# GAT attention weights from per-node exponentials gathered with the rows, in place of scores on TensorE

## The chip, the cores and the metric

The kernel runs on one core of a Trainium2 chip. The metric is the device time of one execution in microseconds (us), as the median of several runs. The engines are called PE (TensorE), DVE (VectorE), ACT (ScalarE), POOL (GpSimd) and SP (SyncE, which only issues DMAs here). All arithmetic of the tensors named below is in float32.

## What is computed

Four graph layers follow each other on x of shape (8, 2048, 128), with one adjacency matrix of 2048 x 2048 whose entries are 1 with probability 1/128, so that a node has 16 neighbours on average. Layers 0 and 1 are transformer blocks with attention over the neighbours. Layers 2 and 3 are GAT layers, and the change is in these:

```python
def _L2_gnn_ref(x, adj, W, a_src, a_dst, ln_gamma, ln_beta):   # _L3_gnn_ref is the same
    h = x @ W
    s_i = h @ a_src
    s_j = h @ a_dst
    e = s_i[:, :, None] + s_j[:, None, :]
    e = jnp.where(e >= 0, e, NEG_SLOPE * e)          # NEG_SLOPE = 0.2
    e = jnp.where(adj[None, :, :] == 0, -jnp.inf, e)
    att = jax.nn.softmax(e, axis=-1)
    att = jnp.nan_to_num(att, nan=0.0)
    out = jnp.einsum('bij,bjd->bid', att, h)
    y = out + x
    mu = jnp.mean(y, axis=-1, keepdims=True)
    var = jnp.mean((y - mu) ** 2, axis=-1, keepdims=True)
    return ln_gamma * (y - mu) * jax.lax.rsqrt(var + LN_EPS) + ln_beta
```

The weight of neighbour j for node i is the exponential of a leaky ReLU of s_i + s_j, divided by the sum of these over the neighbours.

## The kernel before

A first stage (`start`) finds the neighbours of every node and ranks the nodes by their number of neighbours. The 2048 nodes are then worked on in 16 tiles of 128 nodes of nearly equal degree. `CAPS` holds how many neighbour slots each tile has, from 30 down to 11; a slot that a node does not need is called padding. There are 277 slots in all.

For each layer there is a table in HBM with one row per node that holds what its neighbours need from it for all eight batches. For a GAT layer the row has 8 x 128 values of h and then 8 values s_j, 4128 bytes. One **gather** (L296, issued by POOL) brings the rows of one slot for the 128 nodes of a tile, each into its own partition of a kv buffer. A padding slot has an index past the end of the table (2N and more), and its row is skipped.

A GAT layer works on **chunks** of up to four slots of one tile (`pieces(t, 4)`), 75 per layer. `gat_chunk` is a generator; each `yield` ends one of its stages:

1. PE adds up the scores in PSUM: the mask of the padding slots (L654), s_i of the node itself (L658) and the gathered s_j (L662). ACT takes the exponential of the score (L667, tile wa) and of 0.2 times the score (L668, tile wb).
2. DVE takes the maximum of both, which is the exponential of the leaky ReLU: into a PSUM tile `pair` for DVE's own use (L670) and, for the last two batches, into an SBUF tile ws for ACT (L675).
3. DVE multiplies the rows of six batches by their weights (L681, one input in PSUM); ACT does the other two batches (L686).
4. DVE adds the second half of the slots to the first (L690); then PE adds the rows into the tile's accumulator by matmuls with the identity (L696).

Tile 0 has nodes with more neighbours than the others; two extra slots of that tile are shared out over idle partitions ("folded") and brought back by the matrices `spread` and `merge`.

When the last chunk of a tile is done, its **tail** starts: the sums of the weights and their reciprocals (`reciprocal_sums`, L388 to L395), the scaled output (L565), the residual (L706 to L714), the normalisation (`normed`: squares on ACT, L404; a power on POOL, L409; a scale on ACT, L413), and either the projection to the next layer's table row (`project`, L443 to L466) with its scatter by POOL (`put_rows`, L417), or in layer 3 a scale and a shift on DVE (L731, L732) and a store by POOL (L734). Tails are generators too, advanced by one stage in each `slot()`.

Every engine works through its instructions in the order in which the program issues them. That order is written out in `layer`. In iteration i a GAT layer issues the gathers of chunk i + 3, then the scores of chunk i + 1, the products of chunk i - 1, a slot, the maxima of chunk i, a slot, the addition and the matmuls of chunk i - 2, and a slot. Six kv buffers are used in turn, so the gathers of chunk i + 3 go into the buffer of chunk i - 3 and wait until its matmuls are done. A layer's first gathers wait for the last rows of its table.

After layer 3 `verdict` checks on DVE that no list overflowed and no sum left its range. If one did, a general path (`general_path`) computes everything anew.

Of the kernel before, what the change touches and what calls it, by code (L numbers as in the profile page):

```python
# [17 lines left out]
P = 128  # L18
# [11 lines left out]
CHUNK = 4 * NB * (D + 1)  # L30
KVB = 6
AHEAD = 3
# [10 lines left out]
SUM_MIN, SUM_MAX = 1e-25, 1e30  # L43

# [19 lines left out]
def sparse_path(ctx: ExitStack, tc: tile.TileContext, ins: dict, out: bass.AP, flag: bass.AP):  # L64
# [69 lines left out]
    lmask_bf = const.tile([P, sum(CAPS)], BF16, name="lmask_bf")  # L134
    first = [sum(CAPS[:t]) for t in range(NT)]
    s_own = const.tile([P, NT, B], F32, name="s_own")
# [142 lines left out]
    def width(l):  # L279
        return NB * (2 * D if l < 2 else D + 1)  # L280

    tables = [dram.tile([N, width(l)], F32, name=f"table{l}") for l in range(4)]
# [12 lines left out]
    def gather(l, at, dst):  # L295
        nc.gpsimd.indirect_dma_start(  # L296
            out=dst, out_offset=None, in_=tables[l][:, :],
            in_offset=bass.IndirectOffsetOnAxis(ap=lists[:, at : at + 1], axis=0),
            bounds_check=N - 1, oob_is_err=False,
        )  # L300
# [24 lines left out]
    def find_lists(t):  # L325
# [18 lines left out]
        if t == 0:  # L344
# [19 lines left out]
        nc.vector.tensor_copy(lmask_bf[:, sl], lmask[:, sl])  # L364
# [3 lines left out]
            far[:, :s], top[:, :s], 0.0, float(2 * N), op0=ALU.is_equal, op1=ALU.mult  # L368
# [54 lines left out]
    def project(l, i, xT, rows, t):  # L423
# [18 lines left out]
        else:  # L442
# [22 lines left out]
            nc.scalar.copy(rows[:, NB * D + i : NB * D + i + 4], ps[:, :, 0])  # L465
            nc.scalar.copy(s_own[:, t, i : i + 4], ps[:, :, 1])  # L466
# [177 lines left out]
    def gat_chunk(l, c):  # L644
        box, t, k, ns = c["box"], c["t"], c["k"], c["ns"]
        if k == 0:
            box["acc"] = pacc.tile([P, NB // 4, 512], F32, tag="acc", name="acc")
            at, n = (0 if t % 2 == 0 else 512 - NB * CAPS[t]), CAPS[t]
            box["w"] = pair[:, at : at + NB * n].rearrange("p (s b) -> p s b", b=NB)
        acc, w = box["acc"], box["w"]  # L650
        hs = c["buf"]
        e = misc()[:, : ns * NB].rearrange("p (s b) -> p s b", b=NB)
        at = first[t] + k
        nc.tensor.matmul(  # L654
            e, ident_bf, lmask_bf[:, at : at + ns, None].to_broadcast([P, ns, NB]),
            start=True, stop=False,
        )
        nc.tensor.matmul(  # L658
            e, spread if c["folded"] else ident, s_own[:, t, None, :].to_broadcast([P, ns, NB]),
            start=False, stop=False,  # L660
        )
        nc.tensor.matmul(e, ident, hs[:, :, NB * D :], start=False, stop=True)  # L662

        wc = w[:, k : k + ns, :]
        wa = small.tile([P, 4, NB], F32, tag="wa", name="wa", bufs=3)
        wb = small.tile([P, 4, NB], F32, tag="wb", name="wb", bufs=3)
        nc.scalar.activation(wa[:, :ns, :], e, AF.Exp)  # L667
        nc.scalar.activation(wb[:, :ns, :], e, AF.Exp, scale=SLOPE)  # L668
        yield
        nc.vector.tensor_max(wc, wa[:, :ns, :], wb[:, :ns, :])  # L670
        if c["folded"]:
            box["wf"] = small.tile([P, FOLD, NB], F32, tag="wf", name="wf", bufs=1)
            nc.vector.tensor_max(box["wf"], wa[:, :ns, :], wb[:, :ns, :])
        ws = small.tile([P, 4, SCALED], F32, tag="ws", name="ws", bufs=3)
        nc.vector.tensor_max(  # L675
            ws[:, :ns, :], wa[:, :ns, NB - SCALED :], wb[:, :ns, NB - SCALED :]
        )
        yield
        hv = hs[:, :, : NB * D].rearrange("p s (b c) -> p s b c", b=NB)
        nv = NB - SCALED  # L680
        nc.vector.tensor_mul(  # L681
            hv[:, :, :nv, :], hv[:, :, :nv, :], wc[:, :, :nv, None].to_broadcast([P, ns, nv, D])
        )
        for i in range(ns):
            for b in range(nv, NB):
                nc.scalar.mul(hv[:, i, b, :], hv[:, i, b, :], ws[:, i, b - nv : b - nv + 1])  # L686
        yield
        left = -(-ns // 2)
        if ns > 1:
            nc.vector.tensor_add(hv[:, : ns - left], hv[:, : ns - left], hv[:, left:ns])  # L690
        yield
        if c["folded"]:
            folded_sums(box["wf"], box)
        for i in range(left):
            for j in range(NB // 4):
                nc.tensor.matmul(  # L696
                    acc[:, j, :], merge if c["folded"] else ident, hv[:, i, 4 * j : 4 * j + 4, :],
                    start=k + i == 0, stop=c["last"] and i == left - 1,
                )
        yield  # L700
# [41 lines left out]
    def start():  # L742
# [164 lines left out]
        for i in (3, 4, 5):  # L907
            nc.scalar.copy(bufs[i], nil.to_broadcast([P, CHUNK]))


    def verdict():
        ok = small.tile([P, 4], F32, tag="ok", name="ok", bufs=1)
# [7 lines left out]
        nc.vector.tensor_mul(ok[:, 0:1], ok[:, 0:1], ok[:, 2:3])  # L920
        pk = misc()
# [40 lines left out]
    def layer(l):  # L962
# [36 lines left out]
        for i in range(AHEAD):  # L999
            fetch(i)  # L1000
# [22 lines left out]
        if not att:  # L1023
            go(0)
        for i in range(n + 2):
            fetch(i + AHEAD)
# [24 lines left out]
            else:  # L1051


                go(i + 1)
                if is_last(i - 1):
                    sums(l, chunks[i - 1]["t"], chunks[i - 1]["box"])
                go(i - 1)
# [3 lines left out]
                go(i - 2, 2)  # L1061
                if is_last(i - 2):
                    end(i - 2)
# [534 lines left out]
```

## Time and profile before

| What | Value |
|---|---|
| median of 3 runs | 3482.68 us |
| lowest and highest | 3482.06 and 3488.56 us |
| the profiled execution, its own time | 3489.46 us |
| its span, first to last instruction | 3487.7 us |
| busy share of the span | PE 81%, DVE 87%, ACT 42%, POOL 61% |
| moved by DMA | 955.38 MB, mean 274 GB/s |
| layer 2, its gathers under way | 2325 to 2852 us |
| layer 3, its gathers under way | 2903 to 3425 us |

A row of the list of groups names the line of the kernel, the engine, the operation and its tiles (out<-in) with their shapes and the count; then come the busy time in us and the mean of one instruction in ns, and then the idle time of the engine just before these instructions, with what ended it. A row of the timeline has the start and the duration in us, and in brackets the idle time before. A row of the waits has the total in us, how many times, and the longest. "issue" is time in which an engine waited for nothing that the profile shows.

### The profile page before, as it was taken

The page shows a single profiled execution, that of the slowest core. Times are in us where ns is not written, and L with a number is a line of the kernel's source. Part 1 is how long each engine was busy: PE and PEld are TensorE (multiplying, and loading weights), DVE is VectorE, ACT ScalarE, POOL GpSimd, SP SyncE. Part 2 cuts the span into 40 slices and gives each one's busy share as a digit, 9 for nine tenths or more (in the row PEclk, how much of TensorE's full clock was granted, in tenths as well). Part 3 has the DMA queues.
Part 4 walks back from the last instruction along what each step waited for, and adds up shares of the span by engine and source line. Part 5 has one row for each costly group of instructions (what it writes and reads, how often), then busy time and mean ns, then how long its engine had stood idle before and what let it go on. Part 6 is the DMA issues. An engine that isn't in the chain of part 4 may idle for free. (4 is left out here: it accounts for less than half of the span.)

```text
span 3487.7 us, 36421 instructions
## 1 busy us (share of the span) xinstructions
PE 2838.8 (81%) x11364; PEld 1678.0 (48%) x11364; DVE 3033.3 (87%) x2545; ACT 1451.0 (42%) x5142; POOL 2117.5 (61%) x1441
## 2 busy tenths in 40 slices
PE   5657888889899966888888999958889895778786
PEld 4523454555555542445545555644555553434343
DVE  7789999999999839999999999928787764888885
ACT  5712333344444430233333344444555553444444
POOL 0054666666666432656666766537777755888874
PEclk9878999999999989999999999988999997988888
DMA  8486788878787457777887887638989856888883
GB/s 335 183 303 244 278 304 303 322 281 317 294 319 290 182 213 252 290 290 287 302 320 290 306 305 283 240 131 281 313 302 310 313 201 220 286 287 294 290 276 119
DMA packets 195892, 955.38 MB, mean 274 GB/s; under 512 B 33778, under 2 KB 35572, under 8 KB 124080
## 3 DMA queue, kind: packets, MB, share of 16 engines
q0 software_dynamic: 172352, 859.22, 69.0%
q1 hardware_dynamic: 18434, 75.51, 5.7%
q10 hardware_dynamic: 4904, 18.24, 1.4%
q8 instruction: 93, 1.52, 0.2%
q14 instruction: 109, 0.89, 0.1%
HBM read 934.86 MB, written 85.07 MB: 292 GB/s over the span
## 5 line engine op out<-in xcount | busy, mean ns | idle before, releaser
L296 POOL DMA_INDIRECT kv<-table,lists x1108 | 1614.4, 1457 | 553.9 <-issue 225.5
L546 PE MATMUL acc<-kv,ident 128*128 128x512 f32 x2200 | 1112.2, 636 | 255.7 <-DVE kv L536 255.5
L546 PEld LDWEIGHTS acc<-kv,ident 128*128 128x128 f32 x2200 | 414.2, 202 | 699.2 <-issue 370.4
L522 DVE TENSOR_TENSOR kv<-kv,q 128x2048 f32<-128x2048 f32 (+1 forms) x282 | 629.2, 2231 | 71.3 <-DMA kv<-table,lists 64.1
L525 DVE TENSOR_REDUCE sc<-kv 128x128 f32<-128x2048 f32 (+1 forms) x284 | 634.1, 2233 | 9.4
L409 POOL TENSOR_TENSOR rs<-ss,half 128x4 f32<-128x4 f32 x192 | 322.4, 1679 | 517.2 <-ACT n L404 510.0
L536 DVE TENSOR_TENSOR kv<-kv,w 128x2048 f32<-128x2048 f32 (+1 forms) x284 | 631.4, 2223 | 0.0
L696 PE MATMUL acc<-kv,ident 128*128 128x512 f32 x1184 | 605.6, 659 | 15.2 <-DVE kv L690 15.2
L404 ACT ACTIVATE n<-m,eps 128x128 f32<-128x128 f32 x768 | 271.5, 368 | 476.3 <-PE m L628 217.3
L681 DVE TENSOR_TENSOR kv<-kv,pair 128x3072 f32<-128x3072 f32 (+1 forms) x150 | 465.1, 3100 | 0.0
L531 ACT ACTIVATE w<-sc,lmask 128x64 f32<-128x64 f32 x554 | 164.4, 348 | 530.6 <-DVE sc L525 420.1
L696 PEld LDWEIGHTS acc<-kv,ident 128*128 128x128 f32 x1184 | 239.9, 213 | 272.1 <-issue 226.7
L690 DVE TENSOR_TENSOR kv<-kv 128x2048 f32<-128x2048 f32 (+1 forms) x150 | 296.5, 1977 | 85.3 <-ACT kv L686 83.3
L686 ACT ACTIVATE kv<-kv,ws 128x128 f32<-128x128 f32 x1108 | 339.1, 398 | 0.1
L413 ACT ACTIVATE n<-m,rs 128x128 f32<-128x128 f32 x768 | 218.3, 368 | 103.0 <-POOL rs L409 102.5
L667 ACT ACTIVATE wa<-m 128x32 f32<-128x32 f32 (+1 forms) x150 | 29.4, 196 | 494.2 <-PE m L662 494.2
L662 PE MATMUL m<-kv,ident 128*128 128x32 f32 (+1 forms) x300 | 62.1, 289 | 172.7 <-DMA kv<-table,lists 168.5
L404 ACT ACTIVATION_READ_ACCUMULATOR n<-m,eps 128x1 f32 x768 | 159.1, 207 | 0.0
L628 PE MATMUL m<-w_L_w,hT 128*128 128x128 f32 x1024 | 156.3, 275 | 0.0
L670 DVE TENSOR_TENSOR pair<-wa,wb 128x32 f32<-128x32 f32 (+1 forms) x150 | 29.9, 200 | 144.6 <-ACT wb L668 131.8
L417 POOL DMA_INDIRECT table<-rows,perm x48 | 77.8, 1620 | 110.1 <-ACT rows L441 51.6
L662 PEld LDWEIGHTS m<-kv,ident 128*128 128x128 f32 x300 | 49.2, 206 | 178.8 <-issue 150.1
(217 smaller groups left out, 3592.9 us busy)
## 6 DMA issues: line engine op xcount, KB each, us to landing
kept<-xT SPq DMA_DIRECT2D x48, 512.0 KB, 6.2
xT<-kept SPq DMA_DIRECT2D x48, 512.0 KB, 6.3
kv<-table,lists POOLq DMA_INDIRECT x1108, 6.5
kv<-in_adj_dram SPq DMA_DIRECT2D x16, 1024.0 KB, 7.0
table<-kv ACTq DMA_DIRECT2D x16, 1024.0 KB, 5.8
kv<-in_x_nodes_dram SPq DMA_DIRECT2D x16, 512.0 KB, 6.4
found<-cand POOLq DMA_DIRECT2D x16, 64.0 KB, 3.2
table<-rows,perm POOLq DMA_INDIRECT x48, 6.9
```

The source lines that it names most:

```text
L296: nc.gpsimd.indirect_dma_start(out=dst, out_offset=None, in_=tables[l][:, :], in_offset=bass.IndirectOffsetOnAxis(ap=lists[:, at : at + 1] ...
L404: nc.scalar.activation(dst[:, i, :], z[:, i, :], AF.Square, bias=eps, scale=D**-0.5, accum_out=ss[:, i : i + 1],)
L409: nc.gpsimd.tensor_tensor(rs, ss, half, op=ALU.pow)
L413: nc.scalar.mul(dst[:, i, :], z[:, i, :], rs[:, i : i + 1])
L522: nc.vector.tensor_mul(kk, kk, q[:, None].to_broadcast([P, ns, NB, D]))
L525: nc.vector.tensor_reduce(sc[:, :ns].rearrange("p s (b h) -> p (s b) h", h=NH), kk.rearrange("p s b (h j) -> p (s b) h j", h=NH), axis=AX. ...
L536: nc.vector.tensor_mul(vv, vv, w[:, k : k + ns, :].rearrange("p s (b h) -> p (s b) h", h=NH)[:, :, None, :] .to_broadcast([P, ns * NB, HD, ...
L546: nc.tensor.matmul(acc[:, j, :], merge if c["folded"] else ident, kv[:, i, 4 * j : 4 * j + 4, D:], start=k + i == 0, stop=c["last"] and i ...
L681: nc.vector.tensor_mul(hv[:, :, :nv, :], hv[:, :, :nv, :], wc[:, :, :nv, None].to_broadcast([P, ns, nv, D]))
L686: nc.scalar.mul(hv[:, i, b, :], hv[:, i, b, :], ws[:, i, b - nv : b - nv + 1])
L690: nc.vector.tensor_add(hv[:, : ns - left], hv[:, : ns - left], hv[:, left:ns])
L696: nc.tensor.matmul(acc[:, j, :], merge if c["folded"] else ident, hv[:, i, 4 * j : 4 * j + 4, :], start=k + i == 0, stop=c["last"] and i = ...
```

## The change

The exponential of a sum is a product of exponentials. Divided by exp(s_i), which is the same in all weights of a node and so drops out of the softmax, the weight is the larger of exp(s_j) and exp(0.2 s_j) exp(-0.8 s_i). The change puts exp(s_j) and exp(0.2 s_j) into the table row (8 + 8 values in place of 8, so 4160 bytes) and keeps exp(-0.8 s_i) of each node in SBUF (`own`). A chunk then multiplies the second gathered half by `own` on DVE and takes the maximum; PE and ACT have no part in the weights. The projection makes the exponentials, and `score` keeps the raw scores, so that `verdict` can check that none is beyond 80.

There is no mask any more. A padding slot now has the index N, and for the GAT tables row N exists, is filled with zeros once in `start`, and is read like any other row. In layers 0 and 1 row N is still past the end and skipped.

The chunk has one stage less, so the order in `layer` is new as well: in iteration i the gathers of chunk i + 4 are issued, then the maxima of chunk i, a slot, its products, a slot, the addition and the matmuls of chunk i - 1, and a slot.

```diff
-CHUNK = 4 * NB * (D + 1)
+CHUNK = 4 * NB * (D + 2)
-AHEAD = 3
+AHEAD = (3, 3, 4, 4)
+SCORE_MAX = 80.0
...
-    lmask_bf = const.tile([P, sum(CAPS)], BF16, name="lmask_bf")
-    s_own = const.tile([P, NT, B], F32, name="s_own")
+    own = const.tile([P, NT, B], F32, name="own")
+    score = const.tile([P, 2, NT, 2 * B], F32, name="score")
...
-        return NB * (2 * D if l < 2 else D + 1)
-    tables = [dram.tile([N, width(l)], F32, name=f"table{l}") for l in range(4)]
+        return NB * (2 * D if l < 2 else D + 2)
+    tables = [dram.tile([N + (l > 1), width(l)], F32, name=f"table{l}") for l in range(4)]
...
-            bounds_check=N - 1, oob_is_err=False,
+            bounds_check=N - (l < 2), oob_is_err=False,
...
-        nc.vector.tensor_copy(lmask_bf[:, sl], lmask[:, sl])
-            far[:, :s], top[:, :s], 0.0, float(2 * N), op0=ALU.is_equal, op1=ALU.mult
+            far[:, :s], top[:, :s], 0.0, float(N + 1), op0=ALU.is_equal, op1=ALU.mult
...
-            nc.scalar.copy(rows[:, NB * D + i : NB * D + i + 4], ps[:, :, 0])
-            nc.scalar.copy(s_own[:, t, i : i + 4], ps[:, :, 1])
+            at = NB * D + i
+            nc.scalar.activation(rows[:, at : at + 4], ps[:, :, 0], AF.Exp)
+            nc.scalar.activation(rows[:, at + NB : at + NB + 4], ps[:, :, 0], AF.Exp, scale=SLOPE)
+            nc.scalar.activation(own[:, t, i : i + 4], ps[:, :, 1], AF.Exp, scale=SLOPE - 1)
+            nc.scalar.copy(score[:, l - 2, t, 2 * i : 2 * i + 8], ps.rearrange("p b c -> p (b c)"))
...
     def gat_chunk(l, c):
         box, t, k, ns = c["box"], c["t"], c["k"], c["ns"]
+        mine = own[:, t, :]
+        if c["folded"]:
+            pf = misc()[:, :NB]
+            nc.tensor.matmul(pf, spread, mine, start=True, stop=True)
+            mine = small.tile([P, NB], F32, tag="mine", name="mine", bufs=1)
+            nc.scalar.copy(mine, pf)
+            yield
...
-        e = misc()[:, : ns * NB].rearrange("p (s b) -> p s b", b=NB)
-        at = first[t] + k
-        nc.tensor.matmul(
-            e, ident_bf, lmask_bf[:, at : at + ns, None].to_broadcast([P, ns, NB]),
-            start=True, stop=False,
-        )
-        nc.tensor.matmul(
-            e, spread if c["folded"] else ident, s_own[:, t, None, :].to_broadcast([P, ns, NB]),
-            start=False, stop=False,
-        )
-        nc.tensor.matmul(e, ident, hs[:, :, NB * D :], start=False, stop=True)
-
         wc = w[:, k : k + ns, :]
-        wa = small.tile([P, 4, NB], F32, tag="wa", name="wa", bufs=3)
-        wb = small.tile([P, 4, NB], F32, tag="wb", name="wb", bufs=3)
-        nc.scalar.activation(wa[:, :ns, :], e, AF.Exp)
-        nc.scalar.activation(wb[:, :ns, :], e, AF.Exp, scale=SLOPE)
-        yield
-        nc.vector.tensor_max(wc, wa[:, :ns, :], wb[:, :ns, :])
+        wa, wb = hs[:, :, NB * D : NB * (D + 1)], hs[:, :, NB * (D + 1) :]
+        nc.vector.tensor_mul(wb, wb, mine[:, None, :].to_broadcast([P, ns, NB]))
+        nc.vector.tensor_max(wc, wa, wb)
...
         nc.vector.tensor_max(
-            ws[:, :ns, :], wa[:, :ns, NB - SCALED :], wb[:, :ns, NB - SCALED :]
+            ws[:, :ns, :], wa[:, :, NB - SCALED :], wb[:, :, NB - SCALED :]
         )
...
+        for l in (2, 3):
+            nc.sync.dma_start(tables[l][N : N + 1, :], bufs[5][:1, : width(l)])
...
     def verdict():
-        ok = small.tile([P, 4], F32, tag="ok", name="ok", bufs=1)
+        ok = small.tile([P, 5], F32, tag="ok", name="ok", bufs=1)
+        every = score.rearrange("p a t b -> p (a t b)")
+        nc.vector.tensor_reduce(ok[:, 3:4], every, axis=AX.X, op=ALU.max)
+        nc.vector.tensor_reduce(ok[:, 4:5], every, axis=AX.X, op=ALU.min)
+        nc.vector.tensor_single_scalar(ok[:, 3:4], ok[:, 3:4], SCORE_MAX, op=ALU.is_le)
+        nc.vector.tensor_single_scalar(ok[:, 4:5], ok[:, 4:5], -SCORE_MAX, op=ALU.is_ge)
+        nc.vector.tensor_mul(ok[:, 3:4], ok[:, 3:4], ok[:, 4:5])
...
+        nc.vector.tensor_mul(ok[:, 0:1], ok[:, 0:1], ok[:, 3:4])
...
-        for i in range(AHEAD):
+        for i in range(AHEAD[l]):
...
-        if not att:
-            go(0)
         for i in range(n + 2):
-            fetch(i + AHEAD)
+            fetch(i + AHEAD[l])
...
-                go(i + 1)
+                if i + 1 < n and chunks[i + 1]["folded"]:
+                    go(i + 1)
                 if is_last(i - 1):
                     sums(l, chunks[i - 1]["t"], chunks[i - 1]["box"])
-                go(i - 1)
+                go(i)
                 slot()
                 go(i)
                 slot()
-                go(i - 2, 2)
-                if is_last(i - 2):
-                    end(i - 2)
+                go(i - 1, 2)
+                if is_last(i - 1):
+                    end(i - 1)
                 slot()
```

More of the change, by code (lines that the diff above doesn't have):

```diff
@@ L651, in gat_chunk @@
         hs = c["buf"]
-        e = misc()[:, : ns * NB].rearrange("p (s b) -> p s b", b=NB)
-        at = first[t] + k
-        nc.tensor.matmul(
-            e, ident_bf, lmask_bf[:, at : at + ns, None].to_broadcast([P, ns, NB]),
-            start=True, stop=False,
-        )
-        nc.tensor.matmul(
-            e, spread if c["folded"] else ident, s_own[:, t, None, :].to_broadcast([P, ns, NB]),
-            start=False, stop=False,
-        )
-        nc.tensor.matmul(e, ident, hs[:, :, NB * D :], start=False, stop=True)
-        wc = w[:, k : k + ns, :]
-        wa = small.tile([P, 4, NB], F32, tag="wa", name="wa", bufs=3)
-        wb = small.tile([P, 4, NB], F32, tag="wb", name="wb", bufs=3)
-        nc.scalar.activation(wa[:, :ns, :], e, AF.Exp)
-        nc.scalar.activation(wb[:, :ns, :], e, AF.Exp, scale=SLOPE)
-        yield
-        nc.vector.tensor_max(wc, wa[:, :ns, :], wb[:, :ns, :])
+        wc = w[:, k : k + ns, :]
+        wa, wb = hs[:, :, NB * D : NB * (D + 1)], hs[:, :, NB * (D + 1) :]
+        nc.vector.tensor_mul(wb, wb, mine[:, None, :].to_broadcast([P, ns, NB]))
+        nc.vector.tensor_max(wc, wa, wb)
         if c["folded"]:
             box["wf"] = small.tile([P, FOLD, NB], F32, tag="wf", name="wf", bufs=1)
-            nc.vector.tensor_max(box["wf"], wa[:, :ns, :], wb[:, :ns, :])
+            nc.vector.tensor_max(box["wf"], wa, wb)
         ws = small.tile([P, 4, SCALED], F32, tag="ws", name="ws", bufs=3)
         nc.vector.tensor_max(
-            ws[:, :ns, :], wa[:, :ns, NB - SCALED :], wb[:, :ns, NB - SCALED :]
+            ws[:, :ns, :], wa[:, :, NB - SCALED :], wb[:, :, NB - SCALED :]
         )
```

## The prediction

> **What bounds the kernel now.** Only the two GAT layers (l = 2, 3) are changed, so I first looked for their stretches. The table by window gives each engine's busy time, then the DMA share and GB/s. The second and third rows below are the layers while their gathers run (layer 2: 2325 to 2852 us, layer 3: 2903 to 3425 us); between and after them come the tails that close a layer.
>
> ```profile
> core 0: us, PE busy (x) PEld busy (x) DVE busy (x) ACT busy (x) POOL busy (x), PEclk, DMA share, GB/s
> 2325.00:2852.00 527.00, 445.44 (x1801) 260.98 (x1802) 403.65 (x366) 268.78 (x1103) 391.14 (x316) 0.91 0.87 298
> 2903.00:3425.00 522.00, 390.73 (x1216) 205.43 (x1215) 434.23 (x417) 237.01 (x985) 419.85 (x329) 0.86 0.86 287
> ```
>
> The obvious reading is the page's list of groups, where PE waits for gathers and ACT waits for PE's scores:
>
> ```profile
> L667 ACT ACTIVATE wa<-m 128x32 f32<-128x32 f32 (+1 forms) x150 | 29.4, 196 | 494.2 <-PE m L662 494.2
> L662 PE MATMUL m<-kv,ident 128*128 128x32 f32 (+1 forms) x300 | 62.1, 289 | 172.7 <-DMA kv<-table,lists 168.5
> ```
>
> It suggests that the scores are the brake. But a gather that lands late may have been issued late, so I read POOL, which issues every gather, in order of time (start, duration, and in brackets the idle time before), beside DVE:
>
> ```profile
> 3098.08 1.02 POOL L296 DMA_INDIRECT kv<-table,lists  x1 [0.30 <-issue]
> 3099.41 1.00 POOL L296 DMA_INDIRECT kv<-table,lists  x1 [0.30 <-issue]
> 3100.71 1.00 POOL L296 DMA_INDIRECT kv<-table,lists  x1 [0.30 <-PE acc L696]
> 3102.01 2.92 POOL L296 DMA_INDIRECT kv<-table,lists  x1 [0.30 <-issue]
> 3105.24 1.00 POOL L296 DMA_INDIRECT kv<-table,lists  x1 [0.30 <-issue]
> ```
> ```profile
> 3098.15 3.35 DVE L681 TENSOR_TENSOR kv<-kv,pair 128x3072 f32<-128x3072 f32 x1
> 3101.60 0.20 DVE L670 TENSOR_TENSOR pair<-wa,wb 128x32 f32<-128x32 f32 x1
> 3101.71 0.16 DVE L675 TENSOR_TENSOR ws<-wa,wb 128x8 f32<-128x8 f32 x1
> 3101.78 2.29 DVE L690 TENSOR_TENSOR kv<-kv 128x2048 f32<-128x2048 f32 x1
> ```
>
> Two things are to be seen. The gap before every POOL instruction is 0.30 us whatever is named as releaser: that is issue cost, not waiting. So POOL's true load is busy time plus 0.30 us per instruction: layer 3, 419.9 + 329 x 0.30 = 518.6 of 522 us (99%); layer 2, 391.1 + 316 x 0.30 = 485.9 of 527 us (92%). **POOL is full in layer 3 and nearly full in layer 2.** And the gather that starts inside the add L690 (both inputs in SBUF) takes 2.92 us instead of 1.00, while those under L681 (one input in the PSUM tile pair) are not stretched. In layer 2 POOL does wait, for a buffer:
>
> ```profile
> POOL kv L296 <- PE acc L696: 27.8, 21, 5.1
> ```
> ```profile
> L296 POOL DMA_INDIRECT kv<-table,lists x277 | 336.9, 1216 | 118.6 <-issue 59.1 <-PE acc L696 27.8 <-PE m L658 13.3
> ```
> ```profile
> L296 POOL DMA_INDIRECT kv<-table,lists x277 | 359.8, 1299 | 87.3 <-issue 55.7 <-PE acc L696 9.7 <-DMA table<-rows,perm 4.7
> ```
>
> The last two rows are layers 2 and 3; the mean gather is 83 ns longer in layer 3, because a POOL that never waits meets more of the adds.
>
> **What the Trainium skill says.** *SBUF — State Buffer*, "Who interferes with whom": a Vector instruction with two SBUF inputs and a GpSimd instruction that reads SBUF exclude each other. The trace agrees (2.92 against 1.00 us). *ScalarE: Activation LUTs*, "What ACT_TABLE_LOAD costs": a change to another table set costs some 2.66 us. The trace has a single table load, with Exp, Square and Relu all in use, so more Exps cost no load. *DMA: Bandwidth & Descriptors*, "Latency and other measured facts": rows that alias on HBM fell from 207 to 103 GB/s; I use it below for rows read from one address; no run here shows that case.
>
> **The change part by part.** Each layer has 75 chunks and 277 gathers.
>
> *PE and ACT lose the scores.* 150 x (0.18 + 0.28 + 0.29) us, L654, L658 and L662, is 112 us of PE. 150 x 2 x 0.196 is 59 us of ACT. The large effect is that their queues no longer stop for a gather with tails behind them. PE was 445 of 527 us busy in layer 2, so its buffers come free sooner.
>
> *DVE gains a multiply.* It is 128x32 like L670, 0.20 us, and about 0.10 us until the dependent max (the step from L681's end to L670): 150 x 0.30 = 45 us. DVE then stands at 404 + 22 of 527 and 434 + 22 of 522 us, under POOL: no cost. DVE now waits for the gather itself, and the add of the chunk before, outputs, and the last layer's scale and shift are queued behind; PE's sums and POOL's stores wait for those. But a gather is issued four chunks ahead, about 28 us, and lands in 6.0 us (median in both windows), so that wait should be empty.
>
> *The multiply and POOL.* It too has two SBUF inputs. Bounds: all of it lengthens the add's lock, 75 x 0.30 = 22 us a layer; or none, because max and ws, which now run ahead of each add, will stand apart from it. I take 3 us a layer: the multiply replaces them in the run.
>
> *AHEAD 4 and one stage less.* The wait for a free buffer is the same as before: the gathers of iteration i need a matmul of iteration i-1 (chunk i-3 then, i-2 now). What goes is the short time between landing and need. In layer 2 that can return POOL's wait, 527 - 486 = 41 us, less 277 x 0.083 = 23 us of stretch that a full POOL meets: 18 us. I take 14, since the scatter's wait for ACT (6.2 us in that window) stays. In layer 3 there are 3 us to gain: I take 2.
>
> *Padding rows are now read.* About 2048 x 16 = 32,768 of 277 x 128 = 35,456 slots are neighbours; some 2,690 padding slots (7.6%) were skipped and now read row N. Extra per layer: 2,690 x 4,160 B + 32,768 x 32 B = 12.2 MB. At full share the queues move 298/0.87 = 342 and 287/0.86 = 334 GB/s, so layer 2 needs (157.3 + 12.2) MB, 496 us of 527, layer 3 (149.9 + 12.2) MB, 485 us of 522. It still fits under POOL: 0 as taken, up to +100 a layer if one row is slow (rival 1).
>
> *Projections.* Two small ACT copies (0.17 and 0.18) become three Exps and a copy, 4 x 0.19: +0.41 us, 64 times, 26 us on an ACT that is 42% busy. On the path only before the last scatter of layers 1 and 2: +1 us.
>
> *The rest.* Two zero-row stores on SP wait for ACT's fill of bufs[5] (3.6 us); SP has nothing else until layer 0's state stores and POOL refills bufs[5] only for the sixth chunk: 0, at most 3. The folded chunk's spread matmul and copy, once a layer, lie under the first gathers' issue. The verdict's two reductions over 512 elements (0.69 each, as L731) and four small ones lie in DVE's 7.7 us wait before L924. In the closing tails the saved stage and the slower DVE chunk cancel: 0.
>
> Sum: -14 - 2 + 6 + 1 = -9; I add -3 for the first chunks, which skip PE and ACT on the way from landing to DVE: **-12 us**. The profiled execution took 3489.46 us (span 3487.7), 0.19% above the median of 3482.68; the same difference from the median gives 3471 us.
>
> **Rivals.** (1) *Slower: the padding rows make the DMA queues the bound.* The slots fall in the last gathers of each tile, up to 128 reads of one address. They are 21 gathers' worth a layer, 1.6 us each at 342 GB/s. DMA's slack is 31 and 37 us a layer, so it decides once such a read costs more than twice the usual, which is just the fall that the skill's aliased rows show. At three times: 67 - 34 = +33 a layer, near 3540; at four times near 3600. For it: nothing else reads one row so often. Against it: the broadcast load of last_b, 128 reads of one 512 B row, landed in 4.8 us, w_L_wt of the same 64 KB in 7.2. (2) *The gathers' latency, not POOL, was the brake.* Then layers fall to DMA's 496 and 485 us: -68, 3415. For it the 168.5 us above; against it POOL's 99%. (3) *The multiply's lock costs POOL all 22 us a layer.* +44 - 15, about 3505. (4) *The guard trips* and the general path runs: scores of normalised rows against vectors of variance 1/256 are near 0.7, the limit is 80; excluded.
>
> **Numbers.** A measurement of this kernel tells 0.2% (7 us) from no change. My case has 0.50 (own range 3450 to 3488; 0.37 faster, 0.07 within, 0.06 slower), rival 1 0.25, rival 2 0.11, rival 3 0.14 (0.05 within, 0.09 slower). Faster 0.48, same 0.12, slower 0.40. The range 3420 to 3555 leaves out the far ends of rivals 1 and 2.
>
> **What would show it.** Right: POOL's busy time plus 0.30 us per instruction at 97% or more of both layers' gather windows; no DVE wait on gathers in mid-layer; DMA share 0.92 to 0.96; gather mean near 1.30 us in both. Wrong: POOL waiting while the DMA share is near 1 (rival 1), windows near 490 us (rival 2), or a gather mean over 1.37 us (rival 3).

## The result: 0.63% faster, and where the time left

The changed kernel takes 3462.78 us (median of 4 runs, 3460.62 to 3464.90); the kernel before took 3484.41 us beside it (4 runs, 3482.06 to 3488.56). The ratio is 0.9937, with a 95% interval of 0.9919 to 0.9954: faster by 21.6 us. The profiled execution took 3462.36 us (span 3460.6 us) where the one of before had a span of 3487.7 us, so the two traces differ by 27.1 us; the execution of before that was traced lay 5 us above its median. POOL's list of instructions in order of time gives the start of the first and last gather of each layer, which divides that difference:

| stage | before, us | after, us | difference |
|---|---|---|---|
| start to first gather of layer 2 | 2330.2 | 2329.9 | -0.3 |
| layer 2, first to last gather | 513.3 | 488.0 | **-25.3** |
| layer 2's last gather to layer 3's first | 65.9 | 61.0 | -4.9 |
| layer 3, first to last gather | 514.2 | 514.6 | +0.4 |
| layer 3's last gather to the end | 64.0 | 67.0 | +3.0 |

Nearly all of it left in layer 2's gathers; layer 3, with the same change and the same number of gathers, gained nothing. The table by window of the changed kernel, for the two gather windows (busy us of each engine with its instructions, then PE's clock, the DMA share and GB/s):

```profile
core 0: us, PE busy (x) PEld busy (x) DVE busy (x) ACT busy (x) POOL busy (x), PEclk, DMA share, GB/s
2330.00:2819.00 489.00, 391.63 (x1418) 214.79 (x1419) 409.75 (x431) 257.91 (x1001) 393.68 (x315) 0.92 0.94 339
2879.00:3395.00 516.00, 351.48 (x854) 157.53 (x855) 441.50 (x482) 226.53 (x845) 415.36 (x328) 0.86 0.90 309
```

PE lost 47 and 38 us (438.4 and 390.0 us while the gathers were under way before), and in layer 3 that bought nothing. POOL's busy time plus 0.30 us per instruction is now 393.68 + 315 x 0.30 = 488.2 of 489 us in layer 2: what was 92% in the prediction is full. In layer 3 it is 415.36 + 328 x 0.30 = 513.8 of 516 us. (One run below shows that this formula counts POOL's pow, L411, 0.30 us too high; without that both windows stand at 98%, and the prediction's 92% and 99% at 91% and 98%.)

The gathers' rows of POOL's list in those windows, layer 2 and then layer 3 (busy and mean ns, then the idle time before them):

```profile
L299 POOL DMA_INDIRECT kv<-table,lists x277 | 349.5, 1262 | 91.0 <-issue 69.0 <-PE acc L694 7.9 <-PE m L308 4.0
L299 POOL DMA_INDIRECT kv<-table,lists x277 | 350.1, 1264 | 86.9 <-issue 65.7 <-PE acc L694 9.6 <-DMA table<-rows,perm 4.3
```

In layer 2 the idle time before the gathers fell from 118.6 to 91.0 us (the wait for PE's acc matmuls from 27.8 to 7.9), while the gathers themselves grew by 12.6 us. Not more of them were stretched (45 took over 1.15 us, 48 before), but each for longer (2.58 us on average, 2.24 before). In layer 3 the mean fell from 1,299 to 1,264 ns, with 52 stretched gathers in place of 67. The waits of layer 2 (total, times, longest, in us) show ACT waiting for POOL's pow, which in the kernel before came to 2.8 us, and DVE waiting for gathers, where nearly all is its first wait, at the layer's start:

```profile
ACT n L415 <- POOL rs L411: 114.7, 25, 13.2
DVE kv L667 <- DMA kv<-table,lists: 57.4, 6, 53.6
```

The first is the change's side effect. ACT no longer stops for scores and now stops for the one thing that it needs from POOL: the reciprocal root of a tail's norm, queued behind the gathers that were issued ahead.

### The profile page after: what moved, and what is told of

The parts are those of the page before. It is cut to its first block, busy times and chain, and to the rows that moved or that the text cites. A ratio compares the mean times of both kernels' runs of the same rounds, so it can differ in the third digit from the quotient of the medians.

```text
span 3460.6 us, 34591 instructions
## 1 busy us (share of the span) xinstructions
PE 2749.7 (79%) x10618; PEld 1587.6 (46%) x10618; DVE 3055.0 (88%) x2685; ACT 1435.0 (41%) x4972; POOL 2125.4 (61%) x1441
## 2 busy tenths in 40 slices
DMA packets 195887, 980.13 MB, mean 283 GB/s; under 512 B 28334, under 2 KB 30128, under 8 KB 124084
## 5 line engine op out<-in xcount | busy, mean ns | idle before, releaser
L411 POOL TENSOR_TENSOR rs<-ss,half 128x4 f32<-128x4 f32 x192 | 318.2, 1657 | 518.2 <-ACT n L406 517.1
L308 PE MATMUL m<-ident,n 128*128 128x128 f32 x640 | 105.9, 286 | 46.2 <-ACT n L415 45.7
L634 PEld LDWEIGHTS m<-w_L_w,hT 128*128 128x128 f32 x1024 | 135.0, 192 | 0.0
L613 PE MATMUL m<-n1T,w_L_gnn_W 128*128 128x512 f32 x256 | 131.3, 597 | 3.3 <-ACT n1T L608 3.3
L308 PEld LDWEIGHTS m<-ident,n 128*128 128x128 f32 x640 | 81.6, 146 | 103.4 <-ACT n L415 49.9
```

Source lines behind the costliest of these rows:

```text
L411: nc.gpsimd.tensor_tensor(rs, ss, half, op=ALU.pow)
L634: nc.tensor.matmul(y[:, j, :], hT[:, f, j, :], wt["2"][:, f, :], start=False, stop=f == 1, skip_group_check=True,)
```

## Experiments

All times are medians; every ratio is to runs of the kernel before on the same chip. The windows are read as in the table above, each from one trace. The stage ahead of layer 2, which these edits hardly touch, took 2326 to 2334 us in the traces of this document, so a difference of 2 or 3 us in one window means little.

### Is POOL the bound? The pow issued twice, and the padding skipped

```diff
...
+        if gat:
+            junk = small.tile([P, 4], F32, tag="rj", name="rj", bufs=3)
+            nc.gpsimd.tensor_tensor(junk, ss, half, op=ALU.pow)
         nc.gpsimd.tensor_tensor(rs, ss, half, op=ALU.pow)
...
```

> The changed kernel, with POOL's 128x4 pow of the GAT tails issued twice (the second result goes to a tile that nobody reads): 32 more POOL instructions in each of layers 2 and 3, about 26 of them inside a layer's gather window, at 1.11 us busy and 0.30 us issue each. Theory (POOL is the bound of both layers): each gather window grows by 26 x 1.4 = 37 us, to about 525 us in layer 2 and 551 us in layer 3, and the whole by 70 to 85 us, to about 3540 us. Rival (the landing of gathers, DVE's chunk work or the DMA queues set the pace, and POOL is only nearly full): the windows stay within 10 us of 488 and 514.6, the whole within 20 us of 3463.

3511.12 us, ratio 1.0068 (1.0047 to 1.0090): 48 us slower than the changed kernel. Layer 2's window grew by 24.9 us to 512.9, layer 3's by 20.9 to 535.5. That is more than the rival allows and less than I expected, and POOL's list of the doubled kernel in order of time tells why:

```profile
2608.15 2.22 POOL L299 DMA_INDIRECT kv<-table,lists  x1 [0.30 <-issue]
2610.39 1.05 POOL L413 TENSOR_TENSOR rj<-ss,half 128x4 f32<-128x4 f32 x1
2611.42 1.00 POOL L414 TENSOR_TENSOR rs<-ss,half 128x4 f32<-128x4 f32 x1
2612.61 1.07 POOL L299 DMA_INDIRECT kv<-table,lists  x1 [0.18 <-issue]
```

A pow follows its forerunner with no gap to speak of: the 0.30 us belong to the DMA instructions. An added pow costs 1.00 us (its mean in the window was 1,005 ns), 26 of them 26 us, and the windows grew by 24.9 and 20.9: layer 2 passed on 95% of POOL's extra work and layer 3 some 80%. Work added to POOL lengthens both windows, with a little slack in layer 3: POOL sets them. What less work on POOL brings is another question, taken up below.

```diff
-            bounds_check=N - (l < 2), oob_is_err=False,
+            bounds_check=N - 1, oob_is_err=False,
```

> The changed kernel with the gathers' bound lowered by one, so that the reads of row N (the padding slots) are skipped as before the change; this leaves out the zeroing of padding slots, which keep what the buffer held. Theory (POOL is the bound, the padding reads fit under it): the gather windows stay within 4 us of 488 and 514.6, the whole within 6 us of 3463, while the moved bytes fall by some 22 MB and the DMA share of the windows falls from 0.94 and 0.90 to about 0.88 and 0.84. Rival (padding reads cost time, being slow or in the way): each window shrinks by 8 us or more, the whole to 3447 us or less.

This version leaves out the zeros of the padding slots, so those slots add what the buffers held before. 3460.31 us (3459.02 to 3464.70): no change. The bytes fell from 980.13 to 957.49 MB and the DMA share by 0.03 to 0.05, as this table of its windows shows, and the windows stayed (491.0 and 515.2 us from gather to gather). The 22.64 MB are some 2,720 rows of 4,160 bytes a layer. Reading one zero row that often is free here; that it is so because the reads lie under POOL fits both windows.

```profile
2328.00:2820.00 492.00, 391.81 (x1417) 215.04 (x1418) 409.04 (x430) 258.05 (x1001) 396.12 (x315) 0.92 0.91 316
2880.00:3397.00 517.00, 350.69 (x844) 156.54 (x845) 440.96 (x482) 226.63 (x845) 417.94 (x327) 0.86 0.85 289
```

### What gave layer 2 its 25 us? Three parts put back one by one

The change takes work off PE and ACT, drops their place between landing and DVE, and issues gathers four chunks ahead in a new order. I put each back alone in the changed kernel. The scores, unused:

```diff
+        e = misc()[:, : ns * NB].rearrange("p (s b) -> p s b", b=NB)
+        nc.tensor.matmul(e, ident_bf, mask_bf[...], start=True, stop=False)
+        nc.tensor.matmul(e, ident, own[...], start=False, stop=False)
+        nc.tensor.matmul(e, ident, hs[:, :, NB * D : NB * (D + 1)], start=False, stop=True)
...
+        for name in ("ja", "jb"):
+            junk = small.tile([P, 4, NB], F32, tag=name, name=name, bufs=3)
+            nc.scalar.copy(junk[:, :ns, :], e)
```

> The changed kernel with PE's three score matmuls and two small ACT activations per chunk put back, into tiles that nobody reads; PE and ACT again stop for each gather. Theory (layer 2 gained because PE's and ACT's queues no longer stop for gathers and so return buffers sooner): layer 2's gather window goes back to 503 to 515 us and POOL's wait for acc matmuls grows from 7.9 us to 20 us or more; layer 3, where POOL was full before as well, stays within 5 us of 514.6; the whole is 3478 to 3492 us. Rival (the gain of layer 2 comes from the deeper prefetch and the missing stage): both windows within 5 us of the changed kernel, the whole within 8 us of 3463.

3468.70 us (3466.06 to 3474.88), windows 492.9 and 517.1 us. The theory fell: PE and ACT work on the scores of every chunk again, and layer 2 loses some 5 of its 25 us.

```diff
-AHEAD = (3, 3, 4, 4)
+AHEAD = (3, 3, 3, 3)
```

> The changed kernel with gathers issued three chunks ahead in layers 2 and 3 in place of four. Theory (what counts is the work taken off PE's and ACT's queues; a gather lands in some 6 us and a chunk takes 6.5 us, so three chunks ahead is as good as four): both windows within 5 us of 488 and 514.6, the whole within 8 us of 3463. Rival (layer 2 gained from the deeper prefetch): layer 2's window goes back to 500 to 515 us with POOL or DVE waits to match, and the whole to 3475 us or more.

3451.97 us (3448.58 to 3452.73), ratio 0.9890 (0.9858 to 0.9923). The windows are as the theory said, 490.2 and 514.7 us, so depth wasn't it either. But the whole is 10.8 us **faster** than the changed kernel, which neither theory expected (the runs of the two don't overlap); the ends are taken up below.

```diff
...
+        e = misc()[:, : ns * 2 * NB].rearrange("p (s b) -> p s b", b=2 * NB)
+        nc.tensor.matmul(e, ident, hs[:, :, NB * D :], start=True, stop=True)
...
+        nc.scalar.copy(wa, e[:, :, :NB])
+        nc.scalar.copy(wb, e[:, :, NB:])
+        yield
...
-                if i + 1 < n and chunks[i + 1]["folded"]:
-                    go(i + 1)
+                go(i + 1)
```

> The changed kernel in which both gathered exponentials go once through PE (a matmul with the identity, one iteration ahead) and two ACT copies before DVE multiplies and compares them: the trip from landing to DVE over PE's and ACT's queues is back, the rest (four chunks ahead, wide rows, padding reads, multiply) stays. Theory (layer 2 gained because DVE's chunk work no longer waits behind what stands in PE's and ACT's queues): layer 2's gather window goes from 488 back to 503 to 515 us with POOL waiting 20 us or more for acc matmuls, layer 3 stays within 6 us of 514.6, the whole 3478 to 3495 us. Rival (what layer 2 gained came from the new issue order alone): both windows within 6 us, the whole 3460 to 3472 us.

3463.68 us (3463.19 to 3470.35), windows 492.9 and 512.7 us. That theory fell too: DVE waits for PE's and ACT's queues again, and layer 2 keeps some 20 of its 25 us.

### The two halves crossed

No part undid the gain when put back alone, so two parts had to be able to bring it. The last pair of runs crosses them: the kernel before with the new issue order only, four chunks ahead included, and the changed kernel with the old order and three chunks ahead.

```diff
-AHEAD = 3
+AHEAD = (3, 3, 4, 4)
...
-                go(i - 1)
+                go(i)
                 slot()
                 go(i)
                 slot()
-                go(i - 2, 2)
-                if is_last(i - 2):
-                    end(i - 2)
+                go(i - 1, 2)
+                if is_last(i - 1):
+                    end(i - 1)
```

> The kernel before with the new issue order alone: four chunks ahead in layers 2 and 3, maximum and product of a chunk in one iteration, add and matmuls in the next; scores stay on PE, exponentials on ACT, rows narrow, padding skipped. Theory (the issue order brought layer 2's gain: before, three chunks of gathers could be under way for one trip from landing over PE's scores to the acc matmuls that free a buffer, now four): layer 2's gather window falls from 513 to 486 to 497 us and POOL's waits for acc matmuls nearly go, layer 3 stays within 6 us of 514, the whole is 3460 to 3475 us. Rival (scores and exponentials off the queues brought it): layer 2 stays at 505 us or more, the whole 3478 to 3492 us.

> The changed kernel with the old issue order: three chunks ahead, the product one iteration after the maximum, add and matmuls another one later; scores stay gone. Theory (the order alone brought the gain): layer 2's window goes from 488 back to 503 to 515 us with POOL waiting for acc matmuls, the time from its last gather to layer 3's first back to about 65 us, the whole to 3475 to 3490 us. Rival (the loss takes both, PE stopping for a gather and the old order behind it; either remedy is enough): layer 2's window stays at 486 to 497 us, the whole 3455 to 3472 us.

The first took 3462.65 us (3459.46 to 3466.96), ratio 0.9932 (0.9914 to 0.9950); the second, with the same lines the other way and three chunks ahead, 3463.47 us (3455.49 to 3465.36). POOL's waits for the acc matmuls in layer 2's window, in the kernel before with the new order and in the changed one with the old:

```profile
POOL kv L296 <- PE acc L696: 8.3, 18, 1.7
```
```profile
POOL kv L299 <- PE acc L694: 10.0, 18, 1.7
```

| layer 2's window, and the whole, us | scores on PE and ACT | products of exponentials |
|---|---|---|
| old issue order, three chunks ahead | 513.3; 3484.4 (before) | 487.7; 3463.5 |
| new issue order, four chunks ahead | 494.8; 3462.7 | 488.0; 3462.8 (after) |

**The exponentials alone give layer 2's gain, and a reordering of a few lines without them gives 18.5 of its 25 us.** For the first run my theory held and for the second the rival did. Whether the order or the fourth chunk ahead does it in the kernel before was not tried.

That the wholes are alike is in part an accident, since the two rows differ in depth too. At the same three chunks ahead, the new order on top of the exponentials is worth 11.5 us (3451.97 against 3463.47 us): with the old order layer 3's window is 520.4 us, with the new one 514.7. (4.5 us of the difference lie ahead of layer 2 in the traces, where nothing was changed.)

Why did POOL wait in the old order? It could issue chunk i+4 only when the acc matmuls of chunk i-2 were done, and PE gets these last in iteration i, behind the scores of chunk i+1 and the tails' work of the slots. My theory had the landing of chunk i+1 in that queue. The trace of before does not bear it out. POOL had 11 waits of over 0.35 us for acc matmuls there, 21.7 us without the 0.30 us that each issue takes. In the 12 us ahead of them PE never waited for a landing, and shortly before each it had waited 1.1 to 1.7 us for a tail's n from ACT (L305, the transposes of the normalised values). The longest, on POOL and on PE, and PE's waits in mid-layer (2400 to 2840 us):

```profile
2804.74 0.99 POOL L296 DMA_INDIRECT kv<-table,lists  x1 [0.30 <-issue]
2810.80 0.99 POOL L296 DMA_INDIRECT kv<-table,lists  x1 [5.07 <-PE acc L696]
```
```profile
2805.99 1.12 PE L305 MATMUL m<-ident,n 128*128 128x128 f32 x4 [1.69 <-ACT n L413]
2806.90 6.13 PE L696 MATMUL acc<-kv,ident 128*128 128x512 f32 x8
```
```profile
PE m L305 <- ACT n L413: 31.4, 26, 2.0
PE m L662 <- DMA kv<-table,lists: 9.0, 8, 2.8
```

A tail, not a landing, stood ahead of these acc matmuls in PE's queue. PE's wait for ACT can't be all of it: with the exponentials in the old order it came to 44.7 us (2400 to 2815 us), and POOL's wait was nearly gone. That either remedy takes POOL's wait away is measured; how each does it is not shown.

### The ends: how far DVE runs behind POOL

The same two views at the end of layer 3, changed kernel and then three chunks ahead: the last gather on POOL, and the last add on DVE.

```profile
3393.57 0.99 POOL L299 DMA_INDIRECT kv<-table,lists  x1 [0.30 <-issue]
3421.02 1.18 DVE L688 TENSOR_TENSOR kv<-kv 128x1024 f32<-128x1024 f32 x1
```
```profile
3390.17 1.00 POOL L299 DMA_INDIRECT kv<-table,lists  x1 [0.31 <-issue]
3410.24 1.18 DVE L688 TENSOR_TENSOR kv<-kv 128x1024 f32<-128x1024 f32 x1
```

DVE starts its last add 27.5 us after the last gather was issued with four chunks ahead and 20.1 us with three: about one chunk (some 6.5 us) less. All data has long landed; DVE is behind. My explanation was that its add waits for ACT, and ACT for the pow that POOL reaches only after the gathers issued ahead (ACT's 114.7 us above). So I went on to two.

```diff
-AHEAD = (3, 3, 4, 4)
+AHEAD = (3, 3, 2, 2)
```

> The changed kernel with gathers issued two chunks ahead in layers 2 and 3. Theory (in POOL's queue a tail's pow stands behind the gathers issued ahead, so DVE runs that many chunks behind POOL and each layer ends that many chunks after its last gather; four to three brought 4 and 6 us at the two ends): two chunks bring the same again, so the time from the last gather to the next layer's first falls from 57 to about 52 us, the end from 61 to about 55 us, windows within 5 us of 490 and 515, the whole 3436 to 3446 us. Rival (two chunks are about 13 us, too little for the issue of four gathers and a landing of 6 us whenever POOL is late): DVE waits for gathers in mid-layer, the windows grow by 10 us or more each, the whole is 3455 us or more.

3471.76 us (3466.76 to 3477.92). Half of each: the ends shortened as the theory said, to 50.4 and 53.2 us, but the windows grew to 519.9 and 522.4 us as the rival said. DVE's wait for gathers in the middle of layer 2 (2400 to 2780 us), three chunks ahead and then two:

```profile
DVE kv L667 <- DMA kv<-table,lists: 9.3, 11, 2.1
```
```profile
DVE kv L667 <- DMA kv<-table,lists: 69.3, 28, 5.4
```

Three is the best of the depths tried: each chunk of depth costs 4 to 8 us at the end of a layer, and below three DVE waits for landings. Why DVE lags by the depth stays open: the next run takes the pow off POOL, and DVE comes no closer.

### Relief for POOL: the pow on ACT, and no add

```diff
-AHEAD = (3, 3, 4, 4)
+AHEAD = (3, 3, 3, 3)
...
-        nc.gpsimd.tensor_tensor(rs, ss, half, op=ALU.pow)
-        yield
+        if gat:
+            yield
+            lnv = small.tile([P, 4], F32, tag="lnv", name="lnv", bufs=3)
+            nc.scalar.activation(lnv, ss, AF.Ln)
+            nc.scalar.activation(rs, lnv, AF.Exp, scale=-0.5)
+        else:
...
```

> Three chunks ahead, and in the tails of layers 2 and 3 the reciprocal root is exp(-0.5 ln) in two ACT instructions in place of the pow on POOL. Theory (POOL is the bound at 1.00 us for each pow, and ACT's wait for the pow holds DVE back): POOL loses 26 pows in each gather window, so the windows fall by 15 to 26 us from 490.2 and 514.7 (layer 2 no further than its DMA share of 0.95 lets it, 466 us), the ends shorten by 2 to 8 us each, and the whole is 3395 to 3425 us. Rival (ACT reloads its tables for Ln and Exp: 64 changes in each direction on ACT's queue, in front of its part of the chunk's product): no gain, 3450 to 3560 us, with table loads in ACT's list.

3427.80 us (3425.78 to 3437.07), ratio 0.9849 (0.9825 to 0.9873). Both were half right. Against three chunks ahead, layer 3's window fell by 37.7 us to 477.0, more than expected; layer 2's by 4.7 to 485.5; and the ends grew by 6.5 and 9.3 us. ACT does reload its tables, as its list over both windows says:

```profile
L414 ACT ACT_TABLE_LOAD x58 | 74.4, 1283 | 1.0
L415 ACT ACT_TABLE_LOAD x58 | 74.4, 1283 | 1.0
```

The Trainium skill (*ScalarE: Activation LUTs*, "Table sets: the hidden batching unit") lists a set that holds exp and ln together; in this kernel every Ln was still followed by a load for the Exp. In layer 3's window ACT has the room (301 of 478 us busy). At an end the 3.05 us of load, Ln, load and Exp should lie on the path, but at layer 3's end the growth came earlier: DVE had four products of chunks left when the last gather was issued, two with the pow on POOL, and from the last acc matmul to the end it took 33.6 us, 33.4 with the pow on POOL.

```diff
-        if ns > 1:
-            nc.vector.tensor_add(hv[:, : ns - left], hv[:, : ns - left], hv[:, left:ns])
```

> The changed kernel without DVE's add of the chunk's halves, so the second half of every chunk is left out of the sums; PE does the same matmuls. Theory (POOL is the bound, and its gathers are long because they start inside the add's lock): the gather mean falls from 1.26 to 1.00 to 1.05 us, POOL's load by some 65 us a layer, and the DMA queues become the bound: windows of 460 to 478 us in both layers at a DMA share of 0.96 or more, the whole 3370 to 3405 us. Rival 1 (the stretch isn't the add's): the mean stays over 1.2 us and the windows within 8 us of 488 and 514.6. Rival 2 (DVE set the pace and POOL follows it): the windows fall as in the theory but with a gather mean over 1.2 us.

This version leaves out half of each chunk's sum. 3359.35 us (3353.84 to 3360.34), ratio 0.9641 (0.9622 to 0.9661): what the theory said, and 11 us more than its range, with windows of 447.6 and 460.3 us. The gathers' row of layer 2, and the windows:

```profile
L299 POOL DMA_INDIRECT kv<-table,lists x277 | 277.0, 1000 | 107.3 <-issue 72.6 <-PE acc L692 19.8 <-PE m L308 3.9
```
```profile
2331.00:2779.30 448.30, 386.60 (x1413) 213.38 (x1414) 275.88 (x360) 255.88 (x989) 315.55 (x315) 0.92 0.97 368
2838.00:3299.00 461.00, 338.11 (x863) 154.66 (x864) 312.93 (x420) 225.79 (x845) 333.66 (x327) 0.89 0.95 345
```

Without the add a gather of layer 2 takes 1.00 us on average: the 0.26 us of stretch were all the add's. POOL is no longer full, and the DMA share is 0.97 and 0.95. DVE lost its adds too (275.88 us busy in layer 2, 409.75 in the changed kernel), so this run alone doesn't tell how much of the windows' fall is POOL's.

### Two versions that use it

Where PE has room it can sum all four slots of a chunk, so that no add is needed. In fp32, for every fourth chunk of layer 2 and every second of layer 3:

```diff
-AHEAD = (3, 3, 4, 4)
+AHEAD = (3, 3, 3, 3)
+WHOLE = {2: 4, 3: 2}
...
-        left = -(-ns // 2)
-        if ns > 1:
+        left = ns if c["at"] % WHOLE[l] == 1 else -(-ns // 2)
+        if ns > left:
...
```

> Three chunks ahead, all in fp32; for every fourth chunk of layer 2 and every second of layer 3 (19 and 37 chunks) DVE's add is left out and PE sums all four slots instead of two, so the sums are the same. Theory (each add stretches POOL's gathers by 277 x 0.26 / 75 = 0.96 us, and POOL is the bound): windows fall from 490.2 by about 18 us and from 514.7 by about 36 us, the gather mean to about 1.22 and 1.15 us, the whole from 3452 to about 3398 us (3388 to 3415). Rival (four more matmuls of 0.66 us make PE the bound, it is 400 of 491 us busy in layer 2 already): layer 2 gains nothing or loses, POOL waits for acc matmuls, the whole is 3420 us or more.

3416.55 us (3412.37 to 3418.95), ratio 0.9808 (0.9785 to 0.9831). Layer 3 did as the theory said (mean 1.156 us, window down by 36.5 us to 478.2, its gathers 34 us shorter); layer 2's mean fell to 1.185 us, more than expected, but its window only by 3.3 to 486.9 us. Its gathers got 27 us shorter against the mean of 1.284 us with three chunks ahead, and POOL's waits before the scatters and pows took most of it:

```profile
L300 POOL DMA_INDIRECT kv<-table,lists x277 | 328.3, 1185 | 88.0 <-issue 74.4 <-PE acc L695 6.7 <-DMA kv<-table,lists 3.0
L412 POOL TENSOR_TENSOR rs<-ss,half 128x4 f32<-128x4 f32 x27 | 33.2, 1230 | 9.0 <-ACT n L407 7.9 <-issue 0.6
L420 POOL DMA_INDIRECT table<-rows,perm x13 | 17.7, 1361 | 21.1 <-ACT rows L471 18.2 <-DVE kv L680 1.7 <-issue 0.6
```

With three chunks ahead the wait for ACT's rows was 2.2 us and that for ACT's n 1.8 us. The named rival (PE) isn't seen: POOL's 6.7 us for acc matmuls are 23 times the 0.30 us of an issue.

With the products rounded to bf16 the matmul is cheaper and no chunk needs an add; the products go to two half tiles in the place of the sixth gather buffer.

```diff
-AHEAD = (3, 3, 4, 4)
+AHEAD = (3, 3, 3, 3)
...
+        hw = bufs[5].bitcast(BF16)[:, at : at + 4 * NB * D].rearrange(...)
...
-            hv[:, :, :nv, :], hv[:, :, :nv, :], wc[:, :, :nv, None].to_broadcast([P, ns, nv, D])
+            hw[:, :ns, :nv, :], hv[:, :, :nv, :], wc[:, :, :nv, None].to_broadcast([P, ns, nv, D])
...
-        for i in range(left):
+        for i in range(ns):
...
-                    acc[:, j, :], merge if c["folded"] else ident, hv[:, i, 4 * j : 4 * j + 4, :],
+                    acc[:, j, :], merge_bf if c["folded"] else ident_bf, hw[:, i, 4 * j : 4 * j + 4, :],
```

> Three chunks ahead; in layers 2 and 3 the products of a chunk are written as bf16 (DVE and ACT) into two half tiles in the sixth gather buffer's place, five buffers are left for gathers, DVE's add is gone and PE sums all slots with a bf16 identity. Theory (the gathers' stretch under DVE's add is what POOL can get rid of; nothing else reaches the bound before DMA does): gather mean 1.00 to 1.03 us, windows 445 to 465 us with a DMA share of 0.95 or more, ends of 50 to 60 us, the whole 3340 to 3375 us. Rival 1 (twice the matmuls make PE the bound, if one of 128x512 in bf16 takes over 0.5 us): windows over 520 us, the whole over 3480 us. Rival 2 (five buffers are too few): gather mean 1.00 us but POOL waiting for ACT's or DVE's products, windows 470 to 500 us, the whole 3390 to 3440 us.

3373.45 us (3369.91 to 3374.99), ratio 0.9673 (0.9657 to 0.9689): the fastest of the versions that leave nothing out, 2.6% under the changed kernel, at the price of bf16 products. The theory held for the gathers and layer 2 (460.5 us, at a DMA share of 0.94 where 0.95 was named); layer 3's 476.1 us is 11 us over its range and in that of rival 2, though POOL waited there most for ACT's n before its pows, 41.2 us, and 12.9 us for ACT's products. Its windows and the gathers' row of layer 2:

```profile
2329.80:2791.00 461.20, 302.31 (x1382) 180.87 (x1407) 278.87 (x368) 261.58 (x1009) 317.00 (x316) 0.80 0.94 361
2843.80:3321.00 477.20, 259.66 (x829) 117.20 (x845) 316.27 (x421) 227.94 (x845) 334.80 (x328) 0.70 0.92 335
```
```profile
L301 POOL DMA_INDIRECT kv<-table,lists x277 | 277.2, 1001 | 96.2 <-issue 83.3 <-DVE ws L675 8.5 <-ACT kv L690 2.1
```

## Why the prediction came out as it did

The forecast was 3471 us, 12 us less in the profile's terms, with faster as the likeliest outcome; measured were 27 us less in the profile and 21.6 in the medians. Its main reading, that POOL's issue and not the scores sets the GAT layers, is what the pow issued twice showed. That the sum came near is in part luck, since several terms missed both ways. By its steps:

- **Layer 2, -14: the sign was right, the term too small by 11.** POOL's returned wait was put at 41 us, less 23 us of extra stretch, less 4. The stretch was mis-sized: I let layer 2's mean gather rise to layer 3's 1,299 ns, and it rose from 1,216 to 1,262, so 277 x 0.046 = 13 us. The 41 us themselves were about right by luck: the window of 527 us is 14 us longer than the time from first to last gather, and the load counted 0.30 us too much for each of 26 pows. Maximum, ws and the new multiply no longer run into the add, and layer 3's own mean came down. The reason given, that PE's and ACT's queues no longer stop for a gather, is half shown: taking the scores away is enough in the old order, but in the new one they can stay, and PE had stopped for landings only 9.0 us in mid-layer.
- **"The wait for a free buffer is the same as before": wrong.** The prediction counted buffers and found the two orders equal. The kernel before with only the new order, four chunks ahead, gained 18.5 us in that window, so the orders differ: not in which buffer is needed, but in what stands in PE's queue ahead of the matmul that frees it.
- **Layer 3, -2: +0.4.** Right that there was next to nothing to gain.
- **The multiply's lock, +6: not seen.** The gathers' mean fell in layer 3 by 35 ns, 10 us in 277. The window didn't follow: POOL's output stores (L732) took 37.4 us in place of 29.8 in that window, and the rest went into waits. What the multiply costs by itself wasn't tried.
- **First chunks, -3:** the first acc matmul of layer 2 starts 18.3 us after its first gather, before 23.9 us; layer 3 18.4 and 23.8, so 5.4 to 5.6 us each. They are inside the windows, and layer 3's shows that they don't add up with POOL's work: the term should have been nothing.
- **Closing tails, 0: -4.9 and +3.0,** near nothing together, but two effects that cancel. Three chunks ahead brings 3.9 and 6.2 us at the two ends, so the deeper prefetch costs about 10 us there, and the rest of the change brings about as much and a little more. The prediction looked for what the deeper prefetch gains in the windows, found a landing of 6 us against 28 us of lead, and didn't ask how far DVE would then run behind the last gather.
- **Padding rows, 0: right.** The bytes grew by 24.75 MB (predicted 2 x 12.2), and skipping the rows moved nothing. The doubt over one row read often (*DMA: Bandwidth & Descriptors*, "Latency and other measured facts", aliased rows) isn't borne out: layer 2's queues moved 339 GB/s at a share of 0.94 with these reads and 316 at 0.91 without.
- **The signs it named:** POOL at 97% or more in both windows, yes; no DVE wait for gathers in mid-layer, yes; DMA share 0.94 and 0.90 where 0.92 to 0.96 was named, so missed in layer 3; gather mean 1.26 us where 1.30 was named, a miss as well. Rival 2's sign, a window near 490 us, did come in layer 2, but with POOL full, so it could not tell the two apart.

The rivals: padding as the bound is refuted by skipping it. Latency as the brake is refuted for layer 3, and nothing speaks for it in layer 2: POOL did wait there, but for acc matmuls behind a tail, not behind a landing. The lock's 22 us a layer didn't come; its +44 - 15 on 3482.68 make some 3512 us, where the forecast has about 3505.

**What stays open** is layer 2's next bound. Putting the pow on ACT, or dropping a quarter of the adds, took 27 to 30 us off POOL there (26 pows of 1.16 us, 277 gathers of 0.10 us) and gave 3 to 5 us. POOL's own waits took most of it back. The scatter of a tile's rows (`put_rows`) waited for ACT, first with three chunks ahead, then with the pow on ACT:

```profile
POOL table L419 <- ACT rows L470: 2.2, 1, 2.2
```
```profile
POOL table L425 <- ACT rows L476: 29.6, 8, 7.5
```

With a quarter of the adds gone it was 18.2 us, as shown above. The gathers stand behind such a scatter in POOL's queue. What makes a tail's rows late was not tried. The DMA queues were at a share of 0.95 in both runs and at 0.97 with all adds gone, where layer 2 gained 40 us, so 0.95 isn't a fixed ceiling.

## What to carry to other kernels

Before pricing a change by the work it removes, ask which queue is full: here 38 us less of PE in layer 3 were worth nothing, and a reordering of a few lines with a chunk more of prefetch was worth as much as the whole change. When several edits come together, cross them (each alone in the old kernel, each taken back in the new), and keep everything else equal, the depth of the prefetch too: put back one at a time, neither would have been seen here. Before blaming a landing for a wait, look at what the engine in between waited for. And a deeper prefetch can have a price: here the engine that uses the data fell behind by as many chunks as were fetched ahead, and each layer ended that much later.

## What the hardware showed that I had not expected

- A gather of 128 rows takes 1.00 us of POOL, and in layer 2 its stretch to 1.26 us on average came wholly from DVE's add with two SBUF inputs: mean 1,000 ns without the add. That add cost POOL some 72 us a layer (277 x 0.26).
- The 0.30 us before POOL's DMA instructions is theirs alone; the pow that follows a gather starts within 0.02 us in the timeline shown, and a second pow too, while the gather after a pow waits 0.18 us.
- In the version with bf16 products the granted clock of PE was 0.80 and 0.70 in the two windows, where the changed kernel had 0.92 and 0.86. PE was busy 302.31 of 461.20 us in layer 2 there; what the lower clock cost can't be read from this run.
- A change of ACT's tables for a single 128x4 Ln took 1.28 us, with the Ln following 0.01 us later and the load back 0.02 us after it: the 2.66 us for a change that the skill's page states (*ScalarE: Activation LUTs*, "What ACT_TABLE_LOAD costs", the load and a drain) did not appear here.
